# A graph layer and a masked attention layer on one core: block products for the neighbours, one operation for mask and maximum

## The chip, the core and the metric

The kernel runs on one core of a Trainium2 chip. A core has a matrix engine (TensorE, in the profile PE, its weight loads PEld), a vector engine (VectorE, DVE), a scalar engine (ScalarE, ACT), a general engine (GpSimd, POOL) and a queue that issues the transfers (SyncE, SP). Each runs its own instructions in order and waits for the others by semaphores. The metric is the device time of one execution in microseconds.

## The reference, cut to what matters

There are 64 graphs of N = 256 nodes with F = 512 features; all is float32.

```python
# layer 0
deg = jnp.sum(adj, axis=-1, keepdims=True)
agg = jnp.einsum('bij,bjf->bif', adj, x) / jnp.maximum(deg, EPS)
out = relu(jnp.einsum('bnf,of->bno', jnp.concatenate([x, agg], axis=2), W))
x = _layernorm(x + out, axis=-1)
# layer 1, 8 heads of 64, mask = adj + adj
q, k, v = (proj(Wq, bq), proj(Wk, bk), proj(Wv, bv))
scores = jnp.einsum('bhqd,bhkd->bhqk', q, k) * SCALE
attn = jax.nn.softmax(scores * mask, axis=-1)
ctx = jnp.einsum('bhqk,bhkd->bhqd', attn, v)
x = _layernorm(x + jnp.einsum('bse,fe->bsf', ctx, Wo) + bo, axis=-1)
```

The factor 2 of the mask and the scale are folded into the query weights (`QSCALE`), so that the scores are multiplied by `adj` alone.

## The kernel before

A graph's 256 nodes are two tiles of 128 rows (`NT = 2`), its 512 features four chunks. The layer-0 product is turned round: `x W` is computed first, for both halves of W, into the tile `oy` (index 0: the node's own part; index 1: the part `y` that goes to the neighbours), and then `adj y` is divided by the degree and added.

**Products of blocks.** The large products L (`x W`), Q (queries and keys), V (values) and O (output) use a scheme of Winograd's kind: both factors are cut into 2 x 2 blocks, and seven products of blocks take the place of eight. In `winograd`, `product` makes the steps `L1` to `L7` (and so on), which add up in three PSUM banks a, b and c; `kept` makes `Lk5`, `Lk1`, `Lk6`, `Lk4`, which copy a partial sum out of its bank as it stands, and `joined` makes `Lj3`, `Lj2`, `Lj7`, which add one to a part already written. A later product on a bank waits until the partial sum before it has been read. The sums of blocks on the left are made on GpSimd (steps `xS1`-`xS4`, `yS`, `cS`).

**Neighbours.** Step `AY` is the product `adj y`, without that scheme: per tile t two matmuls of 128 x 128 by 128 x 512 into a bank of its own. `AYa` is two VectorE operations: bank times 1/degree plus `oy[:, 0]`, then relu plus x. `AYb`, `AYp`, `AYn` are the layer norm (statistics on VectorE, three small operations on GpSimd, the scaling on ScalarE). `aT` is the transposed `adj`, turned in 32 x 32 blocks on VectorE from the load `Dza`; `xT` comes in the same way from `Dzx`. `Dway`, `Dz1` and `x1T` send the normed x to DRAM, read it back, and turn it for Q and V; `Drest` reads it for the residual, to which `bo` adds the output bias on GpSimd.

**Attention.** The heads go in pairs a, b, c, d. `Sa` is the scores of a pair, into two banks. `ma` multiplies them by `adj`: two VectorE operations of 128 x 512, from PSUM into the tile `sa`. `Ma` is the negated maximum of each row: one VectorE reduction over 128 x 1024. `ea` and `fa` are the exponentials on ScalarE, with the negated maximum as bias and the row sum as a second output; `ra` and `na` divide; `Ta` turns blocks of 32 x 32; `Dwa` and `Dsa` take the weights through DRAM, which completes the transposition; `C0a` (pair a), `C0b` (pair b), `C1a` (pair c), `C1b` (pair d) multiply by v, and `c0`, `c1` copy the context out. `lb`, `lp`, `ln` are the last layer norm and `Dout` the result.

**The order of the work** is written out by hand. `START` lists the steps of the first graphs (name:graph), `PLAN` is one turn of a loop over i = 3 to 59 (name+ahead: the step is made for graph i+ahead), and `END` lists the rest (name:graphs from the end). Every engine gets its instructions in this order. PSUM has eight banks, which all steps take in rotation: a step that takes a new bank waits for the last reader of the bank taken eight before. Most tiles have one buffer only.

Of the kernel before, what the change touches and what calls it, by code (L numbers as in the profile page):

```python
# [35 lines left out]
    AYb1:2 Qk1:1 Q5:1 AYa0:2 nd:0 L5:3 Vj2:1 rc:0 Ta:0 V6:1 nc:0 AYb0:2 Dwa:0 Q6:1 Qj2:1 AYp0:2 Td:0
    Vk6:1 AYp1:2 V5:1 Qk6:1 Tb:0 Dwd:0 L1:3 xS3:3 Vk5:1 yS4:1 Tc:0 Dwb:0 Qk5:1 V7:1 Dwc:0 Q7:1 AYn0:2
    AYn1:2 Q3:1 Qj7:1 Lk1:3 Vj7:1 aT:3 V4:1 deg:3 Dza:4 L6:3 Qj3:1 Dsa:0 Q4:1 Lk6:3 Lk5:3 Dsb:0 Vk4:1
    V3:1 Qk4:1 L7:3 Vj3:1 Drest:0 Dsc:0 Lj7:3 Sa:1 Dsd:0 Sd:1 ma:1 Dway:2 L3:3 Ma:1 md:1 L2:3 ea:1 bo:0
    Lj3:3 fa:1 L4:3 Md:1 Dz1:2 ra:1 Lk4:3 Sb:1 Dadj:4 na:1 Sc:1 mb:1 C0a:0 Lj2:3 fd:1 C1a:0 Mb:1 C1b:0  # L40
    C0b:0 Ta:1 c1:0 eb:1 AY1:3 x1T:2 Dwa:1 Dx:3 c0:0 mc:1 AY0:3 ed:1 yS1:2 Dzx:4 cS3:0 fb:1 O1:0 Wos4:0
    Dadj:5 O2:0 rb:1 yS2:2 aT:4 nb:1 Q1:2 Wos3:0 Mc:1 Q5:2 rd:1 yS4:2 Ok1:0 Qk1:2 AYa1:3 yS3:2 V1:2
    cS1:0 Qk5:2 Tb:1 Q6:2 cS2:0 ec:1 cS4:0 xT1:4 Dwb:1 Q3:2 AYb1:3 Vk1:2 Qk6:2 xT0:4 AYp1:3 O6:0 AYa0:3
    xS1:4 fc:1 V6:2 xS3:4 V5:2 Vk6:2 rc:1 Ok6:0 Q7:2 nc:1 O5:0 Vk5:2 nd:1 Q2:2 Ok5:0 Qj7:2 AYb0:3 O7:0
    Tc:1 AYp0:3 V7:2 xS2:4 O3:0 Oj2:0 Dwc:1 Oj7:0 Q4:2 Vj7:2 Qj3:2 Qj2:2 O4:0 Qk4:2 V3:2 Ok4:0 Oj3:0
    V4:2 AYn0:3 Td:1 Vk4:2 Sa:2 AYn1:3 Vj3:2 Dwd:1 Sc:2 ma:2 Dway:3 Sb:2 Drest:1 Dsc:1 mc:2 Sd:2 L1:4
    Dsb:1 Mc:2 lb0:0 Dsa:1 V2:2 Lk1:4 ec:2 lb1:0 L5:4 lp0:0 Dz1:3 mb:2 lp1:0 fc:2 L6:4 Dsd:1 md:2 xS4:4
# [12 lines left out]
    Sd+0 Dzx+3 Ma+0  # L60
    Sc+0 Dout-2
    C0a-1 mb+0 ea+0
    C1a-1 Dza+2 md+0
    C0b-1 fa+0
    C1b-1 Mb+0 Dz1+1 c1-1
    L5+2 c0-1 mc+0 Dx+2 eb+0 cS3-1
    L1+2 Mc+0 xS2+2 cS1-1 ra+0
    L2+2 Md+0 Lk1+2 xS4+2 Lk5+2 cS2-1 aT+2 fb+0
    L6+2 bo-1
    L3+2 Lk6+2 ec+0  # L70
    O2-1 Lj3+2 na+0
    O1-1
    L7+2 Ok1-1 rb+0 x1T+1 ed+0
    O5-1 Lj7+2 yS1+1 nb+0
    O6-1
    V2+1 Ok6-1 Lj2+2
    L4+2 Ta+0
    V1+1 xT1+3 Lk4+2 Dwa+0 fd+0
    Q1+1 deg+2 xT0+3 fc+0
    O7-1 Tb+0 xS1+3  # L80
    AY0+2 Vk1+1 yS2+1 Oj2-1 Qk1+1 Dwb+0 rc+0 Dsa+0 yS4+1 Ok5-1 Oj7-1
    AY1+2 nc+0 rd+0 cS4-1 xS3+3
    V6+1 AYa1+2 yS3+1 nd+0
    V5+1
    O4-1
    O3-1 Ok4-1 Vk6+1 Tc+0 Vk5+1
    Q6+1 Td+0 Dwc+0
    Q5+1 Qk6+1 Vj2+1 Dwd+0 AYa0+2 Drest+0 Dsb+0
    V3+1 Qk5+1
    V7+1 Vj3+1 Dadj+3 Oj3-1  # L90
    Q7+1 Vj7+1 Dsc+0
    Q3+1 Qj7+1 AYb0+2 Dsd+0
    V4+1 lb0-1 AYp0+2
    Q4+1 lb1-1 Vk4+1 lp0-1 AYn0+2 Qj3+1 lp1-1 AYb1+2
    Q2+1 Qk4+1 AYp1+2 ln1-1 Qj2+1
"""
END = """
    Dza:2 Sb:4 xS2:2 AYn1:3 Sa:4 xS4:2 mb:4 Dway:3 Sc:4 Mb:4 Sd:4 C1a:5 mc:4 fb:4 C0a:5 ma:4 ln0:6 C1b:5
    C0b:5 Dz1:3 md:4 L1:2 Ma:4 Dout:6 L2:2 Lk1:2 Dx:2 eb:4 L5:2 Dzx:1 c0:5 x1T:3 c1:5 L6:2 fa:4 cS1:5
    Mc:4 cS2:5 aT:2 O2:5 Lk6:2 bo:5 fc:4 O5:5 O1:5 Lk5:2 L7:2 ea:4 yS1:3 Ok1:5 yS2:3 L3:2 ec:4 Lj7:2  # L100
    Oj2:5 rc:4 V1:3 Lj2:2 nc:4 Lj3:2 L4:2 rb:4 Ok5:5 Md:4 O6:5 Lk4:2 Vk1:3 Q5:3 Ok6:5 fd:4 Tc:4 V6:3
    ed:4 xT1:1 Dwc:4 AY1:2 ra:4 deg:2 na:4 xT0:1 AY0:2 rd:4 xS3:1 AYa1:2 Qk5:3 yS3:3 Q1:3 cS3:5 AYa0:2
    Vk6:3 yS4:3 V5:3 Qk1:3 xS1:1 O7:5 cS4:5 Vk5:3 V7:3 Oj7:5 nd:4 xS2:1 Ta:4 Q6:3 AYb1:2 Q3:3 Qk6:3
    AYb0:2 AYp1:2 Vj7:3 AYp0:2 Td:4 nb:4 O4:5 Q7:3 Ok4:5 Dwd:4 lb1:5 Dwa:4 AYn1:2 lp1:5 V4:3 Qj7:3 Tb:4
    V3:3 Vk4:3 ln1:5 O3:5 Qj3:3 Dwb:4 AYn0:2 Q4:3 Vj3:3 Dsd:4 Oj3:5 lb0:5 Q2:3 Qk4:3 Dza:1 lp0:5 xS4:1
    ln0:5 Dsc:4 Qj2:3 Sa:3 Sb:3 ma:3 Drest:4 Sd:3 Dsb:4 Ma:3 Sc:3 Dadj:1 L1:1 mc:3 fa:3 Dway:2 Mc:3 L5:1
    Dsa:4 Lk1:1 ea:3 mb:3 Dout:5 L6:1 bo:4 ec:3 aT:1 L2:1 ra:3 Lk6:1 Mb:3 Dx:1 Lk5:1 fc:3 md:3 L7:1
    Dz1:2 na:3 Lj2:1 L3:1 Lj7:1 Md:3 L4:1 Lj3:1 fd:3 rc:3 V2:3 eb:3 Vj2:3 C0a:4 deg:1 Lk4:1 C1a:4 ed:3
    x1T:2 C1b:4 C0b:4 nc:3 yS1:2 AY0:1 yS2:2 c0:4 AY1:1 AYa0:1 c1:4 fb:3 cS3:4 Q1:2 AYa1:1 cS1:4 yS4:2
    Q5:2 yS3:2 Qk1:2 Tc:3 AYb0:1 Q2:2 rb:3 AYp0:1 rd:3 nb:3 O1:4 cS2:4 Qj2:2 O5:4 Ok1:4 Qk5:2 Q6:2 Ok5:4  # L110
    Tb:3 O6:4 Ta:3 Qk6:2 Dwb:3 Q3:2 AYb1:1 Dwa:3 nd:3 Dwc:3 Ok6:4 AYp1:1 Q7:2 Qj3:2 cS4:4 AYn0:1 O7:4
    Qj7:2 AYn1:1 Td:3 Sb:2 Q4:2 mb:2 Dsc:3 Oj7:4 Dwd:3 O3:4 Qk4:2 Mb:2 Dsa:3 O4:4 Oj3:4 eb:2 Dway:1
    Ok4:4 Sa:2 Dsb:3 ma:2 V5:2 fb:2 V1:2 Dsd:3 Ma:2 Vk5:2 V2:2 Vk1:2 lb1:4 fa:2 Sd:2 Drest:3 Dz1:1 md:2
    O2:4 ea:2 V6:2 rb:2 Md:2 Vk6:2 C0a:3 nb:2 Oj2:4 V7:2 lb0:4 V3:2 ra:2 lp0:4 Vj7:2 na:2 Vj2:2 C0b:3
    Tb:2 lp1:4 V4:2 Vj3:2 Vk4:2 x1T:1 C1a:3 fd:2 C1b:3 yS1:1 ln0:4 Sc:2 bo:3 ln1:4 mc:2 Q1:1 c0:3 Dout:4
    c1:3 Mc:2 Q5:1 Qk1:1 yS2:1 Dwb:2 cS1:3 Q6:1 cS2:3 Qk5:1 cS3:3 fc:2 yS4:1 O1:3 cS4:3 Q3:1 Qk6:1 Ok1:3
    Ta:2 yS3:1 ec:2 Q7:1 Qj3:1 Dwa:2 ed:2 rc:2 O6:3 Qj7:1 nc:2 Ok6:3 Sb:1 rd:2 mb:1 O7:3 nd:2 Sa:1 Dsa:2
    Mb:1 O5:3 Tc:2 Q4:1 fb:1 Ok5:3 Dwc:2 Oj7:3 ma:1 Qk4:1 O4:3 Ma:1 eb:1 Q2:1 Td:2 ea:1 O2:3 Ok4:3 Dwd:2
    Qj2:1 fa:1 C0a:2 Drest:2 Dsc:2 rb:1 Sc:1 nb:1 ra:1 Sd:1 Dsb:2 mc:1 O3:3 na:1 lb1:3 Dsd:2 Mc:1 lp1:3
# [11 lines left out]
def kernel(  # L131
# [455 lines left out]
    def score_steps(hp, name):  # L587
# [6 lines left out]
        def of(kind, b):  # L594
            return held[f"{kind}{name}", b]
# [186 lines left out]
```

## Time and profile before

| | |
|---|---|
| three runs | 3089.83, 3091.77, 3093.6 us; median 3091.77 us |
| profiled execution | 3093.68 us, of which the profile's span 3091.9 us |
| mean granted TensorE clock | 0.997 of full speed |
| matmul instructions | 17168, a program matmul on float32 shows as two |
| HBM traffic over the span | 308.55 MB read, 201.33 MB written, 165 GB/s |
| first matmul | 15.86 us after the start, when the first weights have landed |

In what follows, a line such as `L530` is a line of the kernel before. A group line has the operation, output and inputs by the program's names, the count, then busy time in all and the mean of one in ns, then the idle time ahead of it on its engine and what ended it.

### The profile page before, as it was taken

Reading aid. Unit: us, or ns where it says so; the run is one execution under the profiler, and the core shown is the slowest. Engines: PE = TensorE matmul, PEld = TensorE weight load, DVE = VectorE, ACT = ScalarE, POOL = GpSimd, SP = SyncE. Lnnn points to the kernel's source line nnn. Section 1 sums busy time; section 2 is a strip of 40 time slices with the busy share of each in tenths; the row PEclk is TensorE's granted clock in tenths of the full one; section 3 lists DMA queues with packets and bytes.
Section 4 is the critical chain, followed back from the end, with each engine's and each line's share of the span. In section 5 each row is a group of like instructions: output and inputs, shape, how many; then the busy total and the mean of one; then the engine's idle time right before and its main releaser. Section 6 shows DMA issues by size and latency. Waiting matters only on the chain.

```text
span 3091.9 us, 51161 instructions
## 1 busy us (share of the span) xinstructions
PE 3057.1 (99%) x17168; PEld 2262.9 (73%) x17168; DVE 2079.8 (67%) x3594; ACT 1713.5 (55%) x4995; POOL 979.9 (32%) x1677
## 2 busy tenths in 40 slices
PE   7999999999999999999999999999999999999997
PEld 4777777677777776777777777777777777777775
DVE  5666666666666666666666666667666666676674
ACT  2555555555555556555555555555555555555564
POOL 3332333332323333323233333232333333322333
PEclk9999999999999999999999999999999999999998
DMA  8466566565665665756656656557566575565665
GB/s 184 123 181 180 150 175 168 160 182 158 159 183 152 171 171 157 184 156 158 185 154 167 174 154 184 160 155 185 156 163 177 150 184 161 159 183 157 160 167 154
DMA packets 494103, 513.34 MB, mean 166 GB/s; under 512 B 113808, under 2 KB 392336, under 8 KB 493840
## 3 DMA queue, kind: packets, MB, share of 16 engines
q1 hardware_dynamic: 493264, 509.02, 61.6%
q8 instruction: 137, 2.24, 0.3%
q10 hardware_dynamic: 576, 1.05, 0.2%
q14 instruction: 126, 1.03, 0.1%
HBM read 308.55 MB, written 201.33 MB: 165 GB/s over the span
## 4 chain that ended last, share of the span: by engine, by line
PE 97%; DMA 2%; DVE 1%; POOL 0%; SPq 0%; issue 0%; ACT 0%; POOLq 0%; DVEq 0%
PE Qa L462 15%; PE La L435 14%; PE Lc L435 7%; PE pc L688 7%; PE Qc L462 7%; PE Oa L435 7%; PE AY L530 7%; PE Va L435 7%; PE Qb L462 4%; PE Oc L435 4%; PE Vc L435 4%; PE Lb L435 4%; PE sca L605 2%; PE scb L605 2%; PE scc L605 2%; PE Ob L435 2%
## 5 line engine op out<-in xcount | busy, mean ns | idle before, releaser
L478 ACT ACTIVATE qk<-Qa,bqk 128x128 f32<-128x128 f32 x768 | 218.8, 368 | 257.1 <-PE Qa L462 257.0
L451 ACT COPY oy<-La 128x512 f32<-128x512 f32 x192 | 112.3, 585 | 429.6 <-PE La L435 429.6
L516 POOL TENSOR_SCALAR mv<-mv 128x1 f32<-128x1 f32 x256 | 55.8, 218 | 915.1 <-DVE mv L511 884.2
L493 ACT COPY v<-Va 128x256 f32<-128x256 f32 x192 | 70.4, 367 | 340.9 <-PE Va L435 340.9
L376 POOL TENSOR_TENSOR cS<-cT 128x256 f32<-128x256 f32 x128 | 94.1, 735 | 460.4 <-ACT cT L704 460.4
L530 PE MATMUL AY<-oy,aT 128*128 128x512 f32 x512 | 230.8, 593 | 0.0
L503 DVE TENSOR_TENSOR h<-Oa,rest 128x256 f32<-128x256 f32 x192 | 81.4, 424 | 213.8 <-PE Oa L435 209.3
L416 DVE TENSOR_TENSOR oy<-Lc,oy 128x512 f32<-128x512 f32 x64 | 44.2, 691 | 253.8 <-PE Lc L435 248.8
L376 POOL TENSOR_TENSOR yS<-x1T 128x256 f32<-128x256 f32 x128 | 93.7, 732 | 335.0 <-DVE x1T L570 335.0
L376 POOL TENSOR_TENSOR xS<-xT 128x256 f32<-128x256 f32 x128 | 94.5, 739 | 305.3 <-DVE xT L341 273.0
L634 ACT ACTIVATE sa<-sa,nmaxa 128x256 f32<-128x256 f32 x256 | 127.0, 497 | 96.0 <-DVE nmaxa L628 92.4
L542 DVE SCALAR_TENSOR_TENSOR oy<-AY,deg,oy 128x512 f32<-128x512 f32 x128 | 94.8, 741 | 122.0 <-PE AY L530 122.0
L584 POOL TENSOR_TENSOR rest<-rest,bo_sb 128x512 f32<-128x512 f32 x128 | 159.6, 1269 | 29.3 <-DMA rest<-way 29.3
L530 PEld LDWEIGHTS AY<-oy,aT 128*128 128x128 f32 x512 | 96.9, 190 | 96.7 <-issue 91.9
L517 POOL TENSOR_TENSOR mv<-mv,neg_half 128x1 f32<-128x1 f32 x256 | 144.3, 564 | 21.3
L435 PE MATMUL La<-W,xT 128*128 128x512 f32 x256 | 122.6, 602 | 15.9 <-DMA W<-in_w0t_dram 15.9
L634 ACT ACTIVATE sb<-sb,nmaxb 128x256 f32<-128x256 f32 x256 | 128.8, 511 | 3.6 <-DVE nmaxb L628 3.6
L462 PEld LDWEIGHTS Qa<-x1T,Wq 128*128 128x128 f32 x1024 | 124.4, 192 | 6.5 <-DVE x1T L570 1.8
L634 ACT ACTIVATE sd<-sd,nmaxd 128x256 f32<-128x256 f32 x256 | 127.2, 501 | 1.7 <-DVE nmaxd L628 1.7
L634 ACT ACTIVATE sc<-sc,nmaxc 128x256 f32<-128x256 f32 x256 | 127.3, 501 | 1.4 <-DVE nmaxc L628 1.4
L462 PEld LDWEIGHTS Qa<-x1T,Wq_sums 128*128 128x128 f32 x1024 | 124.4, 192 | 3.9 <-issue 0.8
L462 PEld LDWEIGHTS Qa<-yS,Wq 128*128 128x128 f32 x1024 | 124.2, 192 | 3.6 <-issue 0.5
(151 smaller groups left out, 8305.1 us busy)
## 6 DMA issues: line engine op xcount, KB each, us to landing
zx<-in_x_dram SPq DMA_DIRECT2D x256, 128.0 KB, 3.7
x<-in_x_dram SPq DMA_DIRECT2D x256, 128.0 KB, 3.4
way<-x SPq DMA_DIRECT2D x64, 512.0 KB, 3.2
z<-way SPq DMA_DIRECT2D x256, 128.0 KB, 2.9
wsa<-sa SPq DMA_DIRECT2D x64, 512.0 KB, 2.6
wsd<-sd SPq DMA_DIRECT2D x64, 512.0 KB, 3.2
wsb<-sb SPq DMA_DIRECT2D x64, 512.0 KB, 3.0
wsc<-sc SPq DMA_DIRECT2D x64, 512.0 KB, 2.7
```

Of the source, the lines that this page charges most:

```text
L376: nc.gpsimd.tensor_tensor(part_of(s, b, [P, 4, 2, P])[:, k], left(b), right(b), op)
L435: nc.tensor.matmul(ps[:, :width].rearrange("p (m o) -> p m o", o=G), lhsT=left(k, b, c), rhs=w(WEIGHTS[k])[:, :, c], start=first and c == ...
L451: nc.scalar.copy(part_l(b, t, n), ps.rearrange("p (m o) -> p m o", m=2))
L462: nc.tensor.matmul(ps.rearrange("p (m j q) -> p m j q", m=2, j=2)[:, m, j], lhsT=wqk(WEIGHTS[k])[:, m, c, j * P : (j + 1) * P], rhs=left_y ...
L478: nc.scalar.activation(part_q(b, t, n)[:, m, j], ps.rearrange("p (m j q) -> p m j q", m=2, j=2)[:, m, j], AF.Identity, bias=bqk[:, m, c : ...
L517: nc.gpsimd.tensor_tensor(mv[:, 1:2], mv[:, 1:2], neg_half, ALU.pow)
L530: nc.tensor.matmul(ps, lhsT=held["aT", b][:, j, t], rhs=held["oy", b][:, 1, j], start=(j == 0), stop=(j == NT - 1),)
L542: nc.vector.scalar_tensor_tensor(h, held[f"AY{t}", b], rdeg, h, ALU.mult, ALU.add)
L584: nc.gpsimd.tensor_tensor(rest, rest, bo_sb, ALU.add)
L605: nc.tensor.matmul(sc(b, j)[:, t], lhsT=qk[d, 0, hp, t * P : (t + 1) * P], rhs=qk[d, 1, hp].rearrange("d (t b m) -> d b t m", t=NT, m=L), ...
L634: nc.scalar.activation(rows(b)[:, r], rows(b)[:, r], AF.Exp, bias=of("nmax", b)[:, r : r + 1], accum_out=of("total", b)[:, r : r + 1],)
L688: nc.tensor.matmul(ps[j * D : (j + 1) * D, hp % 2], lhsT=held["v", b][:, c, h * D : (h + 1) * D], rhs=held[f"sT{name}", b][:, :, c, j * NT ...
```

## The change

The product `adj y` is cut into blocks as the others are: `adj` into its four 128 x 128 blocks, y into 2 x 2 blocks of 128 x 256. Four sums of blocks of `adj` (`aS1`-`aS4`) and four of y (`bS1`-`bS4`) are made on GpSimd, seven products `Y1` to `Y7` go into two banks (`Ya`, and `Ycb`, whose halves hold the sums c and b), and seven VectorE operations `Yk`/`Yj` scale a partial sum by 1/degree and add it to `oy[:, 0]`. `AYr` keeps the relu and the residual of `AYa`. In the attention, the step m is four operations (one for each row of blocks) that multiply by `adj` and reduce the row to its maximum at once, and M only changes the sign, on GpSimd. The three lists are new.

```diff
+    def adj_block(t, j):
+        return lambda b: held["aT", b][:, j, t]
+    def y_block(j, n):
+        return lambda b: held["oy", b][:, 1, j, n * G : (n + 1) * G]
...
+    def small_sum(name, k, of, left, right, op):
+        steps[f"{name}{k}"] = lambda b: nc.gpsimd.tensor_tensor(of(k)(b), left(b), right(b), op)
+    small_sum("aS", 1, adj_sum, adj_block(1, 0), adj_block(1, 1), ALU.add)
+    small_sum("aS", 2, adj_sum, adj_sum(1), adj_block(0, 0), ALU.subtract)
+    small_sum("aS", 3, adj_sum, adj_block(0, 0), adj_block(1, 0), ALU.subtract)
+    small_sum("aS", 4, adj_sum, adj_block(0, 1), adj_sum(2), ALU.subtract)
+    small_sum("bS", 1, y_sum, y_block(0, 1), y_block(0, 0), ALU.subtract)
+    small_sum("bS", 2, y_sum, y_block(1, 1), y_sum(1), ALU.subtract)
+    small_sum("bS", 3, y_sum, y_block(1, 1), y_block(0, 1), ALU.subtract)
+    small_sum("bS", 4, y_sum, y_block(1, 0), y_sum(2), ALU.subtract)
+    def neighbour_product(k, acc, left, right):
+        @step(f"Y{k}")
+        def _(b):
+            name = "Ya" if acc == "a" else "Ycb"
+            ps = bank(name, b) if k in (5, 1) else held[name, b]
+            nc.tensor.matmul(
+                ps[:, G:] if acc == "b" else ps[:, :G],
+                lhsT=left(b),
+                rhs=right(b),
+                start=k in (5, 1),
+                stop=True,
+                skip_group_check=True,
+            )
+    neighbour_product(5, "c", adj_sum(1), y_sum(1))
+    neighbour_product(1, "a", adj_block(0, 0), y_block(0, 0))
+    neighbour_product(3, "c", adj_sum(4), y_block(1, 1))
+    neighbour_product(6, "a", adj_sum(2), y_sum(2))
+    neighbour_product(2, "b", adj_block(0, 1), y_block(1, 0))
+    neighbour_product(7, "a", adj_sum(3), y_sum(3))
+    neighbour_product(4, "a", adj_block(1, 1), y_sum(4))
+    def neighbour_part(name, acc, t, n):
+        @step(name)
+        def _(b):
+            ps = held["Ya" if acc == "a" else "Ycb", b]
+            h = held["oy", b][:, 0, t, n * G : (n + 1) * G]
+            nc.vector.scalar_tensor_tensor(
+                h, ps[:, G:] if acc == "b" else ps[:, :G], held["deg", b][:, t : t + 1], h, ALU.mult, ALU.add
+            )
...
-        @step(f"AY{t}")
-        def _(b):
-            ps = bank(f"AY{t}", b)
-            for j in range(NT):
-                nc.tensor.matmul(
-                    ps,
-                    lhsT=held["aT", b][:, j, t],
-                    rhs=held["oy", b][:, 1, j],
-                    start=(j == 0),
-                    stop=(j == NT - 1),
-                )
-        @step(f"AYa{t}")
+        @step(f"AYr{t}")
         def _(b):
             h = held["oy", b][:, 0, t]
-            rdeg = held["deg", b][:, t : t + 1]
-            nc.vector.scalar_tensor_tensor(h, held[f"AY{t}", b], rdeg, h, ALU.mult, ALU.add)
             nc.vector.scalar_tensor_tensor(h, h, 0.0, held["x", b][:, t], ALU.max, ALU.add)
...
-            tile_of(f"s{name}", b, [P, A, NT, R, L])
+            s = tile_of(f"s{name}", b, [P, A, NT, R, L])
+            nmax = tile_of(f"nmax{name}", b, [P, R], small, "nmax")
             for j in range(2):
-                nc.vector.tensor_tensor(
-                    rows(b)[:, j * NT : (j + 1) * NT],
-                    sc(b, j).rearrange("p t (k l) -> p t k l", l=L),
-                    held["adj", b].rearrange("p t (k l) -> p t k l", l=L),
-                    ALU.mult,
-                )
+                for t in range(NT):
+                    r = j * NT + t
+                    nc.vector.tensor_tensor_reduce(
+                        out=s[:, :, :, r],
+                        in0=sc(b, j)[:, t].rearrange("p (a c l) -> p a c l", a=A, l=L),
+                        in1=held["adj", b][:, t].rearrange("p (a c l) -> p a c l", a=A, l=L),
+                        scale=1.0,
+                        scalar=-3.4028234663852886e38,
+                        op0=ALU.mult,
+                        op1=ALU.max,
+                        accum_out=nmax[:, r : r + 1],
+                    )
         @step(f"M{name}")
         def _(b):
-            nmax = tile_of(f"nmax{name}", b, [P, R], small, "nmax")
-            nc.vector.tensor_reduce(nmax, rows(b), AX.XY, ALU.max, negate=True)
+            nc.gpsimd.tensor_scalar(of("nmax", b), of("nmax", b), -1.0, None, ALU.mult)
```

The new PLAN whole, the old one cut to its first and last lines; the parts of START and END that the prediction speaks of:

```diff
 PLAN = """
-    Sa+0 AYn1+1
-    Sb+0 ma+0 ln0-2 Dway+1
-    Sd+0 Dzx+3 Ma+0
-    Sc+0 Dout-2
-    C0a-1 mb+0 ea+0
-    C1a-1 Dza+2 md+0
-    C0b-1 fa+0
-    C1b-1 Mb+0 Dz1+1 c1-1
-    L5+2 c0-1 mc+0 Dx+2 eb+0 cS3-1
-    L1+2 Mc+0 xS2+2 cS1-1 ra+0
-    L2+2 Md+0 Lk1+2 xS4+2 Lk5+2 cS2-1 aT+2 fb+0
...
-    Q4+1 lb1-1 Vk4+1 lp0-1 AYn0+2 Qj3+1 lp1-1 AYb1+2
-    Q2+1 Qk4+1 AYp1+2 ln1-1 Qj2+1
+    Sa+0 xS4+2 AYn0+1 Dout-2 Md+0
+    Sb+0 aS1+2
+    C1a-1 Dway+1 mc+0 fd+0
+    C0a-1 ma+0 ed+0
+    C1b-1
+    C0b-1 c1-1 mb+0 c0-1
+    L1+2 cS1-1 rd+0 Dz1+1 Mb+0 cS3-1
+    L5+2 Lk1+2 Ma+0 cS2-1 nd+0 bo-1
+    O2-1
+    L6+2 Lk5+2 Td+0
+    O1-1 Mc+0 cS4-1 Lk6+2 Dwd+0 ea+0
+    L2+2 eb+0
+    L7+2 Lj2+2 deg+2 fc+0
+    L3+2 Dsd+0 Ok1-1 Lj7+2 fa+0 x1T+1
+    O5-1 fb+0
+    O6-1 yS1+1
+    L4+2 Ok6-1 ec+0 Lj3+2 Ok5-1 bS1+2
+    Q1+1 Oj2-1 Lk4+2 ra+0 aS2+2 xT1+3 na+0 bS2+2 xT0+3
+    Y1+2 aS3+2
+    O7-1 Dzx+4 xS3+3
+    O3-1 Oj7-1 bS3+2 Yk1+2 Dx+2
+    Q5+1 rc+0 aS4+2 rb+0 nc+0 Oj3-1 yS3+1 Ta+0 Dza+3 yS2+1
+    V1+1 lb0-1
+    O4-1 Qk1+1 lp0-1
+    Y6+2 Ok4-1
+    Q2+1 Yk6+2 nb+0 yS4+1 Tc+0 bS4+2
+    Y5+2 Dwc+0
+    Q6+1 Yk5+2 Drest+0 Vk1+1 Dwa+0 lb1-1 Tb+0
+    Y2+2 Qk6+1
+    Y7+2
+    Y3+2 Qj2+1 Dwb+0
+    V5+1 Dadj+3 Qk5+1 Yj7+2
+    V6+1 Yj3+2 Yj2+2
+    Q7+1 AYr0+2 Vk6+1 Dsc+0 Vk5+1 Dsa+0
+    Y4+2 Qj7+1
+    V2+1 aT+3
+    V7+1 Dsb+0 Yk4+2
+    Q4+1 AYb0+2 AYr1+2 AYp0+2
+    Q3+1 Vj7+1 Qk4+1 AYb1+2 AYp1+2 ln0-1
+    V3+1 lp1-1
+    V4+1 Vj3+1 Qj3+1 Vk4+1
+    Sd+1 xS1+3 Vj2+1 AYn1+2
+    Sc+1 xS2+3 md+1 ln1-1
...
 START = """
+    bS1:0 Wq:0 Y1:0 aS2:0 Lj7:0 Y5:0 aS4:0 Yk1:0 L4:0 bS2:0 Yk5:0 aS3:0 bS3:0 Y6:0 Lk4:0 xT0:1 Y3:0
+    Yk6:0 Y2:0 bS4:0 xT1:1 Y7:0 Yj7:0 xS1:1 Yj3:0 Y4:0 Yj2:0 xS3:1 L2:1 Yk4:0 AYr0:0 bv2:0 AYb0:0 Dadj:1
...
+    bS2:1 Yk5:1 Wqs1:0 bS3:1 Y6:1 Lk4:1 Yk6:1 Dza:2 bS4:1 x1T:0 Y7:1 Y3:1 Y2:1 Dx:1 Wqs2:0 Q1:0 yS1:0
...
 END = """
+    nc:2 C0b:3 Sb:1 ed:2 mb:1 Q4:1 c0:3 Tc:2 Qk4:1 rd:2 Dwc:2 Mb:1 Dsa:2 nd:2 C1a:3 ma:1 C1b:3 Sc:1 c1:3
+    Ma:1 eb:1 cS1:3 O1:3 Td:2 cS2:3 O5:3 fb:1 cS4:3 Ok1:3 O2:3 Dwd:2 mc:1 Dsc:2 cS3:3 fa:1 Sd:1 Ok5:3
+    Dsb:2 V1:1 Mc:1 ea:1 V2:1 Oj2:3 fc:1 O3:3 ra:1 rb:1 O6:3 md:1 Dsd:2 ec:1 Ok6:3 Oj3:3 O7:3 na:1 lb0:3
+    C0a:2 Oj7:3 lp0:3 Md:1 O4:3 nb:1 Ok4:3 C0b:2 rc:1 Drest:2 lb1:3 V5:1 ed:1 Ta:1 lp1:3 C1a:2 ln0:3
...
```

## The prediction

> **What bounds the kernel.** I read the shares of the engines first, then the chain that ended last, then that chain in order of time inside one turn of the loop, then the groups by shape. Shares, and the chain's shares by engine:
>
> ```profile
> PE 3057.1 (99%) x17168; PEld 2262.9 (73%) x17168; DVE 2079.8 (67%) x3594; ACT 1713.5 (55%) x4995; POOL 979.9 (32%) x1677
> ...
> PE 97%; DMA 2%; DVE 1%; POOL 0%; SPq 0%; issue 0%; ACT 0%; POOLq 0%; DVEq 0%
> ```
>
> TensorE carries 97% of the path, so a change elsewhere counts only if it makes TensorE wait. One turn, from one `sca` to the next (columns: length, busy time of PE, PEld, DVE, ACT, POOL, clock, DMA share, GB/s):
>
> ```profile
> 1536.16:1583.66 47.50, 47.50 (x271) 35.31 (x270) 32.20 (x56) 26.74 (x79) 15.06 (x27) 1.00 0.64 166
> ```
>
> Every `sca` in the loop is 47.50 us behind the last. The chain inside a turn (start, length):
>
> ```profile
> 1515.11 0.86 PE Oa L435 x4
> 1515.97 3.43 PE AY L530 x8
> ...
> 1536.16 1.06 PE sca L605 x8
> 1538.09 0.86 PE scd L605 x8
> 1539.82 3.60 PE pc L688 x32
> 1543.42 1.91 PE Lc L435 x4
> 1545.34 1.72 PE La L435 x4
> ```
>
> Products follow without gaps; only the entries to the scores (1.06 for 0.86), to the context (3.60 for 4 x 0.86) and back to L (1.91 for 1.72) cost more, about 0.55 us a turn together. The new PLAN has the same three entries (Sd Sc Sa Sb over the end of the turn, four C, L1), so that part stays.
>
> **The product, on TensorE.** Removed: AY, eight instructions of 512 columns (512 in the trace for 64 batches), 3.43 us, 0.429 each. Added: seven block products of one matmul. Each program matmul shows as two instructions (4 a batch, 512 in all), so 14 of 128x256. The row for that shape is V or O: 0.862 us for four, 0.2155 each, and 14 x 0.2155 = 3.02. Gain 0.414 us a batch, x64 = **26.5 us**. It is an eighth of 3.43 less 0.01: the shape has no overhead of its own. The weight loads do not come out, because they are shorter than what covers them (190 ns against 215):
>
> ```profile
> L530 PE MATMUL AY<-oy,aT 128*128 128x512 f32 x512 | 230.8, 593 | 0.0
> L416 DVE TENSOR_TENSOR v<-Va,v 128x256 f32<-128x256 f32 x64 | 27.1, 423 | 2.9 <-ACT v L493 0.6 <-PE Va L435 0.2
> L618 DVE TENSOR_TENSOR sa<-sca,adj 128x512 f32<-128x512 f32 x128 | 82.4, 686 | 24.2 <-PE sca L605 24.2
> L628 DVE TENSOR_REDUCE nmaxa<-sa 128x4 f32<-128x1024 f32 x64 | 78.0, 1219 | 2.1
> L542 DVE SCALAR_TENSOR_TENSOR oy<-AY,deg,oy 128x512 f32<-128x512 f32 x128 | 94.8, 741 | 122.0 <-PE AY L530 122.0
> L376 POOL TENSOR_TENSOR yS<-x1T,yS 128x256 f32<-128x256 f32 x64 | 48.0, 749 | 4.5
> L516 POOL TENSOR_SCALAR mv<-mv 128x1 f32<-128x1 f32 x256 | 55.8, 218 | 915.1 <-DVE mv L511 884.2
> L530 PEld LDWEIGHTS AY<-oy,aT 128*128 128x128 f32 x512 | 96.9, 190 | 96.7 <-issue 91.9
> ```
>
> **VectorE.** Removed per batch: the eight mask products (327.7/64 = 5.12 us over the four names), the four reductions (309.5/64 = 4.84), two scaled additions from PSUM (1.48): 11.44. Added: seven scaled additions of 256 columns at 0.741 - 0.267 (slope of 512 to 256 in the rows 686 and 423) = 0.47: 3.3; and 16 fused mask-and-maximum operations of 256 columns, which no row shows. Call one u.
>
> Lower end: two 256-column TENSOR_TENSORs end to end in the tail's timeline start at 3045.39 and 3045.72, so u = 0.33 if the maximum is free. Upper end: 0.42, plus 0.27 for a second pass over 256 columns, plus 0.17 (the smallest VectorE row, a 128x4 RECIPROCAL, 166 ns) to write the maximum out: 0.86. I take 0.52, near the 0.42 row with 0.1 for the write-out. 16 x 0.52 = 8.3, so VectorE goes from 32.2 to 32.4 us a turn (29.4 to 37.8 at the ends) of 47.1, all beside TensorE.
>
> [...]
>
> **Where u would show.** The eight PSUM banks go round in order, so a product waits for the mask that frees its bank. From the start of Sd, TensorE reaches C1a at 3.65 us, L1 at 7.25, L5 at 9.07, O2 at 10.8, O1 at 13.4 and L2 at 14.2 (sums of the pieces above). They need 2, 6, 8, 10, 12 and 14 fused operations done, and VectorE can start at about 1.05 (Sd's end; Vj3, Qj3, Vj2 are through by 0.7). L2 is tightest: (14.2 - 1.05)/14 = 0.94. Up to u = 0.94 nothing waits.
>
> **GpSimd.** Added: four bS (128x256, 0.735), four aS (128x128, about 0.735 less half of the 0.53 from 256 to 512 in the rows 735 and 1269, so 0.47), four negations (0.22): 5.7 us, 15.1 to 20.8 of 47.1. M now waits on POOL for the mask, with cS1 and cS3 ahead of Mb and Ma (0.73 each) and cS, bo and bS queued behind; ScalarE's exponentials wait for M. If all of 1.5 us came late, the weights' transfer would take it: Dsb is issued 12.3 us of TensorE work ahead of C0b and needs some 2.2 to issue and 4.7 to land in the tail's rows. So 5 us are spare; beyond that each us late costs a us per turn.
>
> **Chains and moved steps.** A product waits until the part before it in its bank is drained: Y1 to Y6, Y6 to Y7, Y7 to Y4 have 5.2, 4.4 and 3.9 us of other products between them in PLAN; a drain takes 0.47 plus at most 1.2 of a transpose ahead. SP issues the same transfers. Dza and Dzx move up to a turn ahead (13 us between Dza+3 and aT+3, against 7 before, where it waited 12.6 us in all); Dway, Dz1 and x1T keep 10.3 us from Dz1's issue to x1T's place against 11.9, and z landed in 6.2 us at worst in the tail. Cost nil; if a z transfer took over 10 us, Q1 would wait for it.
>
> **Ends.** In START Y4:0 stands directly behind Y7:0 and Y7:1 behind Y6:1: two stops of about 0.6 (0.47 and the hand-over), +1.2. In END 33 products of 0.86 stand behind the last score Sd:1, where 29 stood: 3.4 us more work under the last head's way to the end (49 us before). But three transfers of four DMAs stand ahead of its last one, and ln0 and ln1 ahead of its exponentials; I take half, -1.5.
>
> Sum: -26.5 + 1.2 - 1.5 = -26.8. The profiled execution took 3093.68 (span 3091.9), so 3066.9; the median of the three runs is 1.9 lower, 3091.77, which gives **3065**.
>
> **Rivals.**
> - Slower: the fused operation holds the banks. [...] It decides from u = 0.97. For it: no row of this operation. Against it: it must be over twice the plain product. 6%.
> - The gain is given back: Y4 or Y7 finds VectorE inside a 1.2 us transpose, or x1T comes late, 0.41 us a turn: 3090, no change. For: VectorE is busy two thirds of the turn, and seven drains of 0.47 replace two. Against: 3.9 us of cover at the least. 4%. A part of it, 0.1 to 0.25 a turn, 3071 to 3080: 10%.
> - More than forecast: the end of before lost 4.4 us to the mask of the last head, and the products after it took 1.9 instead of 0.95 at a lower clock:
>
> ```profile
> 3049.38 1.98 PE L688 MATMUL pc<-sTc,v 128*64 128x256 f32 x8 [4.36 <-DVE sd L618]
> 3051.29 1.97 PE L688 MATMUL pc<-sTb,v 128*64 128x256 f32 x8
> 3053.20 1.95 PE L435 MATMUL Vc<-Wv_sums,yS 128*128 128x256 f32 x4
> ```
>
> In END of after, the bank for C1a:2 waits for Oj3:61, listed 4.3 us of TensorE work ahead, not for a mask. If all 7.3 us go in place of 1.5: 3059. 14%.
>
> The forecast itself has 66%, 3061 to 3071. The range 3057 to 3077 takes in the better end and most of the part given back. Runs differ by 0.1%, so 0.2% (6.2 us) is what can be told from no change: faster 90%, same 4%, slower 6%.
>
> **What would show it.** Right: 47.08 us from score to score in the loop, 896 instructions for the new product at 0.2155, no wait of PE for VectorE in mid-run, DVE busy 1900 to 2400 us, POOL near 1340. Wrong: a wait at L2, O2 or L5 ended by the fused mask, Y products longer than 0.43, or a loop at 47.08 with ends that differ by more than 5 us.

## The result, and the profile after

| | before | after |
|---|---|---|
| three runs, median | 3091.77 us | 3069.96 us (3067.2 to 3070.47) |
| profiled execution, of it the span | 3093.68, 3091.9 us | 3069.96, 3068.2 us |
| mean granted TensorE clock | 0.997 | 0.998 |

The ratio is 0.9928, with a 95% interval of 0.9909 to 0.9948: 21.8 us less by the medians, 23.7 by the profiled executions. The forecast was 3065, in a range of 3057 to 3077.

First the page of after: the shares of the engines, and the chain's shares.

```profile
PE 3031.2 (99%) x17552; PEld 2324.1 (76%) x17552; DVE 1897.9 (62%) x5194; ACT 1689.5 (55%) x4995; POOL 1341.2 (44%) x2445
...
PE 98%; DMA 1%; DVE 0%; ACT 0%; SPq 0%; issue 0%; POOL 0%; POOLq 0%; DVEq 0%; ACTq 0%
```

TensorE carries the path as before, with 384 instructions more (896 of the new product for 512 of the old). VectorE lost 182 us of busy time and GpSimd gained 361; neither is on the chain. One turn of the loop, from one `scd` to the next (the columns as in the prediction):

```profile
1528.14:1575.23 47.09, 47.09 (x276) 36.27 (x275) 29.40 (x82) 26.32 (x78) 20.74 (x39) 1.00 0.62 168
```

47.09 us where 47.50 stood, TensorE busy through all of it, VectorE at 29.4 and GpSimd at 20.7. The groups by shape show the new operations one by one:

```profile
L553 POOL TENSOR_TENSOR yB<-oy 128x256 f32<-128x256 f32 x128 | 94.3, 736 | 111.1 <-DVE oy L429 105.5 <-DVE totalb L721 5.3 <-DVE totalc L721 0.2
L593 DVE SCALAR_TENSOR_TENSOR oy<-Ya,deg,oy 128x256 f32<-128x256 f32 x256 | 119.6, 467 | 9.8 <-PE Ya L571 9.1
L690 DVE CUSTOM_DVE_ANT_0 sa<-sca,adj 128x256 f32<-128x256 f32 x256 | 93.0, 420 | 3.1 <-PE sca L674 3.1
L690 DVE DVE_READ_ACCUMULATOR2_ANT nmaxa<- 128x1 f32 x256 | 21.3, 83 | 0.0
L703 POOL TENSOR_SCALAR nmaxd<-nmaxd 128x4 f32<-128x4 f32 x64 | 14.9, 232 | 49.0 <-DVE nmaxd L690 49.0
```

The fused mask and maximum is a `CUSTOM_DVE_ANT_0` of 0.42 us and a read-out of the maximum of 0.08. What counts in a row of sixteen is how they follow each other, and that is in the timeline of VectorE (start, length):

```profile
1529.65 0.42 DVE L690 CUSTOM_DVE_ANT_0 sd<-scd,adj 128x256 f32<-128x256 f32 x1
1530.00 0.09 DVE L690 DVE_READ_ACCUMULATOR2_ANT nmaxd<- 128x1 f32 x1
1530.00 0.42 DVE L690 CUSTOM_DVE_ANT_0 sd<-scd,adj 128x256 f32<-128x256 f32 x1
```

The next operation starts together with the read-out of the one before, 0.345 us after that one's start on the mean of the sixteen (1529.30 to 1534.82).

The loop is as forecast; what is missing lies at its edge. The timeline of TensorE in the first turn (graph 2's context, just behind START):

```profile
211.63 1.08 PE L763 MATMUL pc<-sTd,v 128*64 128x256 f32 x8 [0.43 <-DMA sTd<-wsd]
214.38 1.98 PE L763 MATMUL pc<-sTb,v 128*64 128x256 f32 x8 [1.67 <-DMA sTb<-wsb]
216.28 2.65 PE L448 MATMUL La<-W,xT 128*128 128x512 f32 x4
```

Two waits for the attention weights, 2.1 us, and then products that are too long: 2.65 for an L that takes 1.98 at this place of later turns. That turn lasts 51.19 us (205.59 to 256.78), 4.1 more than the rest; before has no wait there, and its first turn takes 47.50. The chain of waits in order of time says what stood ahead:

```profile
203.19 6.14 DMA rest<-way
209.33 0.02 issue
209.35 4.89 DMA sTb<-wsb
```

`rest` is the residual of the same graph, 512 KB that GpSimd takes up only at 219.49, when it adds the bias. It is issued at 203.19, ahead of the reads of pairs d (203.67) and b (205.91).

The tail has the same pattern, in the timeline of TensorE:

```profile
3045.17 1.08 PE L763 MATMUL pc<-sTc,v 128*64 128x256 f32 x8 [1.46 <-DMA sTc<-wsc]
3049.37 1.97 PE L763 MATMUL pc<-sTd,v 128*64 128x256 f32 x8 [3.12 <-DMA sTd<-wsd]
```

The 4.36 us for the last mask that before shows are gone. In their place stand these two waits for transfers, 0.93 us for a copy of v and 1.43 for a copy of the context.

### The profile page after: what moved, and what is told of

The parts are those of the page before. It is cut to its first block, busy times and chain, and to the rows that moved or that the text cites. A ratio compares the mean times of both kernels' runs of the same rounds, so it can differ in the third digit from the quotient of the medians.

```text
span 3068.2 us, 54922 instructions
## 1 busy us (share of the span) xinstructions
PE 3031.2 (99%) x17552; PEld 2324.1 (76%) x17552; DVE 1897.9 (62%) x5194; ACT 1689.5 (55%) x4995; POOL 1341.2 (44%) x2445
## 3 DMA queue, kind: packets, MB, share of 16 engines
q10 hardware_dynamic: 576, 1.05, 0.2%
## 4 chain that ended last, share of the span: by engine, by line
PE 98%; DMA 1%; DVE 0%; ACT 0%; SPq 0%; issue 0%; POOL 0%; POOLq 0%; DVEq 0%; ACTq 0%
PE La L448 15%; PE Qa L475 15%; PE Qc L475 7%; PE pc L763 7%; PE Oa L448 7%; PE Lc L448 7%; PE Va L448 7%; PE Qb L475 4%; PE Lb L448 4%; PE Ya L571 4%; PE Oc L448 4%; PE Vc L448 4%; PE Ycb L571 3%; PE scd L674 2%; PE Ob L448 2%; PE Vb L448 2%
## 5 line engine op out<-in xcount | busy, mean ns | idle before, releaser
L529 POOL TENSOR_SCALAR mv<-mv 128x1 f32<-128x1 f32 x256 | 77.6, 303 | 769.3 <-DVE mv L524 756.8
L733 DVE STREAM_TRANSPOSE sd<-sd 128x1024 f32<-128x1024 f32 x64 | 79.6, 1244 | 273.4 <-ACT sd L726 273.4
L429 DVE TENSOR_TENSOR oy<-Lb,oy 128x512 f32<-128x512 f32 x64 | 44.2, 691 | 209.3 <-PE Lb L448 202.4
L726 ACT ACTIVATE sc<-sc,totalc 128x256 f32<-128x256 f32 x256 | 109.3, 497 | 106.7 <-DVE totalc L721 106.7
L553 POOL TENSOR_TENSOR yB<-oy 128x256 f32<-128x256 f32 x128 | 94.3, 736 | 111.1 <-DVE oy L429 105.5
L709 ACT ACTIVATE sd<-sd,nmaxd 128x256 f32<-128x256 f32 x256 | 127.0, 497 | 24.5 <-POOL nmaxd L703 24.4
L779 ACT COPY cT<-pc 128x512 f32<-128x512 f32 x128 | 74.9, 586 | 116.3 <-PE pc L763 116.3
L448 PE MATMUL Lb<-W,xT 128*128 128x512 f32 x256 | 122.2, 600 | 15.6 <-DMA W<-in_w0t_dram 15.6
```

Of the source, the lines that this page charges most:

```text
L448: nc.tensor.matmul(ps[:, :width].rearrange("p (m o) -> p m o", o=G), lhsT=left(k, b, c), rhs=w(WEIGHTS[k])[:, :, c], start=first and c == ...
L553: steps[f"{name}{k}"] = lambda b: nc.gpsimd.tensor_tensor(of(k)(b), left(b), right(b), op)
L709: nc.scalar.activation(rows(b)[:, r], rows(b)[:, r], AF.Exp, bias=of("nmax", b)[:, r : r + 1], accum_out=of("total", b)[:, r : r + 1],)
L726: nc.scalar.activation(rows(b)[:, r], rows(b)[:, r], AF.Identity, scale=of("total", b)[:, r : r + 1])
```

## The experiments

Times are set against the kernel before on the same chip: 3092.2 us (31 runs) for e1, e2, e3 and e6, 3090.74 (9 runs) for e4, e5 and e8, 3091.55 (9 runs) for e9, e10 and e11. e4, e5 and e9 are one execution each.

### Is it the product or the mask?

Three kernels take the two halves apart. **e1_old_mask** is after with the mask and the maximum of before:

```diff
-                    nc.vector.tensor_tensor_reduce(out=s[:, :, :, r], ..., op1=ALU.max, accum_out=nmax[:, r : r + 1])
+                nc.vector.tensor_tensor(rows(b)[:, j * NT : (j + 1) * NT], ..., ALU.mult)
...
-            nc.gpsimd.tensor_scalar(of("nmax", b), of("nmax", b), -1.0, None, ALU.mult)
+            nc.vector.tensor_reduce(nmax, rows(b), AX.XY, ALU.max, negate=True)
```

> The changed kernel with the mask and the maximum of before (eight mask products and four reductions a batch on VectorE), product by blocks and lists as changed. Theory (TensorE bounds every turn, the mask part is hidden): 47.09 us from score to score in the loop as in the changed kernel, VectorE busy about 2.6 us a turn more, time within 3 us of the changed kernel's 3070. Rival (relief of VectorE is worth something): the turn goes back toward 47.2 to 47.5 and waits of TensorE for VectorE show at L2 or O2.

3069.18 us (ratio 0.9925, 0.991 to 0.9939), level with after. One turn, in the columns used above:

```profile
1528.14:1575.23 47.09, 47.09 (x278) 36.27 (x276) 33.29 (x61) 26.30 (x79) 19.86 (x35) 1.00 0.63 168
```

VectorE works 3.9 us more in a turn and TensorE doesn't notice. **e2_old_product** is after with AY at the place of Y4, no sums of blocks, and the lists otherwise those of after:

```diff
-    Q5+1 rc+0 aS4+2 rb+0 nc+0 Oj3-1 yS3+1 Ta+0 Dza+3 yS2+1
+    Q5+1 rc+0 rb+0 nc+0 Oj3-1 yS3+1 Ta+0 Dza+3 yS2+1
...
-    Y4+2 Qj7+1
+    AY0+2 AY1+2 Qj7+1
...
-    Q4+1 AYb0+2 AYr1+2 AYp0+2
+    Q4+1 AYa0+2 AYr0+2 AYb0+2 AYp0+2
```

> The changed kernel with the neighbours' product of before (two products of 512 columns a batch, both at the place of Y4, no sums of blocks), mask and lists otherwise as changed. Theory: 47.50 us a turn, 26.5 us more than the changed kernel, 3096 give or take 5. Rival (the new order of steps carries part of the gain): under 3085 and a turn under 47.4.

3097.13 us (ratio 1.0017, 1.0011 to 1.0024):

```profile
1446.94:1494.44 47.50, 47.50 (x270) 35.13 (x269) 28.26 (x77) 26.30 (x78) 16.38 (x31) 1.00 0.62 168
```

The turn is back at 47.50: the seven products are the whole gain of the loop. The run is also 4.9 us slower than before with the same work on TensorE; its first scores of the loop start at 211.67 us, where before has 206.19 and after 205.59. START in the new order thus costs the old product 5.5 us. **e3_mask_alone** is before, lists included, with the fused operation and the sign on GpSimd:

> The kernel before with only the fused mask and maximum and the sign on GpSimd, lists of before. Theory: 47.50 us a turn, 3092 give or take 3, although VectorE is busy some 2.6 us a turn less. Rival (VectorE's relief counts): 47.4 or less a turn, 3085 or less. Other rival (the sign on GpSimd comes late): above 47.6 a turn, with C waiting for sT.

3091.17 us (ratio 0.9995, 0.9986 to 1.0003), the turn still 47.50 (`sca` at 1441.43 and 1488.93). Taken alone, without the product, the mask part changes nothing either.

### How long may the fused operation be?

The prediction said that nothing waits until it takes 0.94 us. **e4_mask_twice** and **e5_mask_thrice** issue each of them two and three times:

```diff
-                    nc.vector.tensor_tensor_reduce(
+                    for _ in range(2):
+                        nc.vector.tensor_tensor_reduce(
```

> The kernel after with each fused mask-and-maximum operation issued twice in a row; the second computes the same again, so nothing else changes. In the trace of after these operations follow each other at 0.345 us, so the pair takes u = 0.69 for each row of blocks, and VectorE rises from 29.4 to about 34.9 us a turn. My theory (PSUM banks bind only from u = 0.94): L2 needs 1.05 + 14 x 0.69 = 10.7 us and comes at 14.2, so nothing waits; turn 47.09, time within 6 us of after's 3070. Rival (a full VectorE delays the chain from the scores to the weights and the scaled additions long before any bank is late): the turn rises by 0.2 us or more, 3082 or above, and TensorE waits for transfers sT or for parts of Y.

> The kernel after with each fused mask-and-maximum operation issued three times in a row, the same result each time; nothing else changes. u = 3 x 0.345 = 1.035, above the 0.94 from which the prediction said that banks bind. My theory: L2 then waits 1.05 + 14 x 1.035 - 14.2 = 1.3 us a turn, ended by the mask, and VectorE is at about 40.5 us a turn; with 57 turns 3070 + 75 to 90 = 3145 to 3160, with the waits of TensorE at L2, O2 or L5 put down to the mask. Rival (the banks have more room than the sum says, since VectorE begins earlier or the pairs' second halves come free sooner): turn 47.1 to 47.3, under 3085. Second rival (the weights' chain is late first): waits at C0 and C1 for the transfers sT, not at L2.

3146.85 us for two and 3696.7 for three. My theory fell twice: two should have cost nothing and took 1.2 us a turn (48.32), and three took 10.4 us in some two turns of three (57.48) and 8.7 in the others (55.79), where some 1.3 to 1.6 was expected. The 1.7 us between the two kinds of turn are a lower clock (0.97 on the mean of the turn for 1.00), shown in the last section. The rival for two had the size and not the place: TensorE waits neither for the transfers nor for parts of Y.

One error was the length. In the timeline of VectorE the operations of e4 start at 1565.44, 1565.91, 1566.26 and 1566.72: one that repeats the one before it starts 0.465 us after it, not 0.345. So u was 0.81 in e4 and 1.28 in e5 (sixteen rows from 1547.56 to 1568.04). That alone doesn't explain e4, for L2 then needs 1.05 + 14 x 0.81 = 12.4 us and comes at 14.3. The waits of TensorE in e4 name another place (us in all, times, longest):

```profile
PE La L448 <- ACT oy L464: 49.8, 57, 1.0
```

Not a bank that the mask holds, but a copy by ScalarE of a part of L. The timeline of ScalarE in e4:

```profile
1578.65 1.70 ACT L728 ACTIVATE sd<-sd,totald 128x256 f32<-128x256 f32 x4 [4.37 <-DVE totald L723]
1580.26 0.56 ACT L464 COPY oy<-Lc 128x512 f32<-128x512 f32 x1
1580.73 0.58 ACT L464 COPY oy<-La 128x512 f32<-128x512 f32 x1
```

ScalarE stood still for 4.37 us in front of the division of pair d (`nd`), which waits for the reciprocal `rd`. On VectorE `rd` is listed behind the four masks. Behind `nd` stand the copies Lk5 and Lk6, whose sources had long been ready and without which the bank can't take its next product. In after `nd` starts 9.8 us behind Sd (1537.95), and in e4 14.4. The waits of TensorE in e5 show both mechanisms:

```profile
PE La L448 <- ACT oy L464: 191.6, 58, 5.0
PE pc L765 <- issue: 84.0, 57, 1.5
PE Lb L448 <- DVE nmaxb L691: 80.4, 56, 1.4
PE Ob L448 <- DVE nmaxa L691: 34.7, 57, 0.7
PE Lc L448 <- DVE nmaxc L691: 26.5, 58, 1.5
```

The banks bind at L5 (`Lc`), O2 (`Ob`) and L2 (`Lb`), the places that the prediction named. The wait of `pc` that has no releaser is a fourth, C0a, which the prediction left out: it takes the second bank of pair d and so needs four operations done. The timelines of VectorE and of TensorE, with the last operation on pair d and C0a:

```profile
356.94 0.42 DVE L691 CUSTOM_DVE_ANT_0 sd<-scd,adj 128x256 f32<-128x256 f32 x1
```

```profile
357.47 1.08 PE L765 MATMUL pc<-sTa,v 128*64 128x256 f32 x8 [1.47 <-issue]
```

C0a starts 0.11 us after the operation's end. The copy behind `nd` costs more than any one bank, 3.3 us a turn; these four banks together cost 3.9. **e9_twice_div_late** puts the new theory to the test:

```diff
-    L5+2 Lk1+2 Ma+0 cS2-1 nd+0 bo-1
+    L5+2 Lk1+2 Ma+0 cS2-1 bo-1
     O2-1
-    L6+2 Lk5+2 Td+0
-    O1-1 Mc+0 cS4-1 Lk6+2 Dwd+0 ea+0
+    L6+2 Lk5+2
+    O1-1 Mc+0 cS4-1 Lk6+2 nd+0 Td+0 Dwd+0 ea+0
```

> The kernel of the run with each fused operation issued twice, with one thing moved in PLAN: the division and the block transposition of pair d (nd and Td) stand behind the copy Lk6 instead of ahead of Lk5. In the run without the move a turn took 48.32 us, and TensorE waited 0.88 us in each for the copy of a part of L. My new theory: the sixteen fused operations last 13.0 us there (0.81 for a pair, not 0.69); the reciprocal rd stands behind them on VectorE, nd on ScalarE waits for rd, and the copies Lk5 and Lk6, which free the bank for the next L, are queued behind nd. With nd moved they no longer wait, no bank is late (L2 needs 1.05 + 14 x 0.81 = 12.4 us and comes at 14.3), and the turn is 47.1 to 47.2 again: 3074 to 3085 in all, since START and END keep their order. Rival (VectorE's 13 us block is late for other work too, the rows' sums on GpSimd or the parts of L that it adds): the wait only goes to another place and the turn stays at 48 us or more, 3130 to 3150.

3082.25 us, 65 less than e4 with the same instructions. It is 12 over after, of which 57 turns make 5; the rest lies in START and END, which keep the order of e4. Its ScalarE timeline and its turn:

```profile
1542.17 0.59 ACT L464 COPY oy<-Lc 128x512 f32<-128x512 f32 x1 [1.08 <-PE Lc L448]
1544.75 0.59 ACT L464 COPY oy<-La 128x512 f32<-128x512 f32 x1 [1.99 <-PE La L448]
1545.46 1.71 ACT L728 ACTIVATE sd<-sd,totald 128x256 f32<-128x256 f32 x4
```

```profile
1531.08:1578.26 47.18, 47.18 (x276) 36.50 (x275) 36.21 (x114) 26.52 (x78) 20.76 (x39) 1.00 0.63 167
```

The copies now wait for TensorE and no longer TensorE for them. With VectorE at 36.2 us a turn and u = 0.81, the turn is back to within 0.09 us, so the order of ScalarE's queue was the cause in e4. The 0.09 us arise ahead of L1, which comes 7.35 us behind Sd where after has 7.26: C0a comes at 4.61 for 4.57, 0.12 us after the fourth operation on pair d has ended, so its bank begins to bind at this u.

### The residual ahead of the weights

**e6_rest_late** moves one transfer of after, behind the pair that it delayed:

```diff
-    lb0:1 Dsc:2 AYr1:4 lp0:1 Dsa:2 V7:3 Qj7:3 V3:3 AYr0:4 Drest:2 Q4:3 Vj7:3 Dsd:2 Qj2:3 AYb1:4 V4:3
-    Qk4:3 Dsb:2 lb1:1 ...
+    lb0:1 Dsc:2 AYr1:4 lp0:1 Dsa:2 V7:3 Qj7:3 V3:3 AYr0:4 Q4:3 Vj7:3 Dsd:2 Qj2:3 AYb1:4 V4:3
+    Qk4:3 Dsb:2 Drest:2 lb1:1 ...
```

> The changed kernel with one step moved in START: the reload of the residual of graph 2 (Drest:2) stands behind Dsb:2 instead of ahead of Dsd:2. Theory (the first turn of the loop lost 4.1 us because the 512 KB reload went ahead of the weights that C1b and C0b wait for): the first turn falls from 51.2 to 47.1 to 48 us, no wait for sTd or sTb there, 3 to 4 us off the whole, about 3066. Rival (that stretch is bound by the traffic of all transfers, whatever their order): the first turn stays at 50 or more, no change in time.

3066.72 us (ratio 0.9915, 0.99 to 0.993). The first turn takes 47.96 us for 51.19, and one of its waits is left, in the timeline of TensorE:

```profile
213.56 1.08 PE L763 MATMUL pc<-sTb,v 128*64 128x256 f32 x8 [0.64 <-DMA sTb<-wsb]
214.58 1.98 PE L448 MATMUL La<-W,xT 128*128 128x512 f32 x4
```

The L behind it has its usual 1.98 us. START came to its end at 206.45, 0.9 us later than in after, but that is within what one kernel shows: e10 below is after unchanged and has 207.06. The other traces agree on the order of the two transfers: with `Drest` ahead the first turn takes 50.30 us in e1 and 49.22 in e10, with it behind 47.08 in e8 and 47.69 in e11. **e8_rest_late_twice** makes the same move in the tail as well:

```diff
-    Ok6:2 Oj2:2 ... Ok4:2 lb0:2 Drest:1 Dsd:1 lb1:2 lp0:2
+    Ok6:2 Oj2:2 ... Ok4:2 lb0:2 Dsd:1 Drest:1 lb1:2 lp0:2
```

> The kernel after with the two residual reads moved in SP's order: the one of graph 2 in START stands behind the transfers of pair b (as in the run with that move alone, 3066.7 us), and the one of the last graph in END stands behind the transfers of the last pair d. In the run with the first move alone, SP issued the last residual read at 3039.09 when VectorE's first layer-norm step let its buffer go, and the four reads of pair d only from 3039.57 to 3041.4, although SP was free at 3038.19; they landed 5.2 us after the last issue and TensorE waited 2.55 us. My theory: the four reads go out 1.4 us earlier and share the engines with no 512 KB read, so that wait falls to about 0.5 to 1.1 us and the run to about 3064.5 to 3065.5, ahead of both kernels. Rival: the residual is then late for the last output sum, or the products after it simply start earlier and wait at the layer norm of graph 2 instead: no change against 3066.7.

3063.49 us (ratio 0.9915, 0.9901 to 0.9929). In the tail, by the timeline of TensorE:

```profile
3041.45 1.08 PE L763 MATMUL pc<-sTc,v 128*64 128x256 f32 x8 [1.19 <-DMA sTc<-wsc]
3043.91 1.65 PE L763 MATMUL pc<-sTd,v 128*64 128x256 f32 x8 [1.38 <-DMA sTd<-wsd]
```

The wait for pair d fell from 2.55 to 1.38 us, not as far as expected. From the start of the last graph's first C to the end it is 23.4 us, where e6 has 26.0. By the ratios e6 and e8 can't be told apart, so the second move alone is shown by the traces only; after and e8 were put on one chip, **e10_after_again** and **e11_late_twice_again**, unchanged:

> The kernel after, unchanged, for a comparison on one chip with the next run. Expected 3068 to 3072 us and a ratio of 0.992 to 0.994 to before.

> The kernel with both residual reads moved behind the transfers that TensorE waits for, on the same chip as the kernel after. By the traces the two moves bring 3.2 us at the seam of START and loop, less 0.9 us of later START, and 2.6 us in the tail, so it should be 4.5 to 6.5 us under the kernel after. Rival (chips and single executions differ by as much): the two are within 2 us of each other.

3068.05 us (3066.78 to 3068.89) and 3064.15 (3063.7 to 3065.66); the ratios to before are 0.9924 (0.9911 to 0.9936) and 0.9913 (0.99 to 0.9927). The version with both moves is 3.9 us faster than after, with no overlap of the five runs each; 4.5 to 6.5 was expected. The two profiled executions differ by 4.7: the first turn by 1.5 (49.22 and 47.69), the tail from the last graph's first C by 2.6 (24.4 and 21.8), the end of START by 0.8. So the tail gave what the traces had promised, and the first turn gave less than the 3.2 us between after and e6. Two waits are left in the tail of e11, in the timeline of TensorE:

```profile
3044.67 1.08 PE L763 MATMUL pc<-sTd,v 128*64 128x256 f32 x8 [1.26 <-DMA sTd<-wsd]
...
3048.94 1.13 PE L448 MATMUL Oc<-Wo_sums,cS 128*128 128x256 f32 x4 [1.26 <-POOL cS L389]
```

The second is for the block sums cS, which are queued behind the bias of the residual on GpSimd (from 3045.71). In e8 it is absent: there the three products ahead took 1.65, 2.07 and 1.21 us for 1.08, 1.13 and 1.03 here, and cS was ready in time. To list the bias behind cS in the tail would be the next step; it wasn't tried.

## Why the prediction was right, and where it was off

The forecast was 26.8 us from the profiled execution, of which 23.7 came. Term by term, from the two traces: a turn is 47.497 us in before and 47.087 in after, on the mean of 56 turns, and of the 64 products five fall into START and two into END.

| term | forecast | measured |
|---|---|---|
| seven products for eight, 64 batches | -26.5 | -26.2 |
| START, two stops | +1.2 | +1.4 |
| first turn of the loop | not in the sum | +4.1 |
| END | -1.5 | -3.0 |
| sum | -26.8 | -23.7 |

- **The product.** Right to 0.01 us a turn: 47.08 forecast, 47.09 measured, and e2 gives 47.50 back. The three entries to scores, context and L stayed in the turn as said, and none of the seven drains is waited for in the loop.
- **START.** The stops came at Y4:0 and Y7:1 as predicted, 0.67 us each. The profile puts the first down to a sum on GpSimd, but VectorE's drain ended 0.15 us before the product began, as at the second.
- **The seam of START and loop** is the term that failed. The prediction worked out that Dsb has 5 us to spare, but from PLAN, where it is issued 12.3 us of TensorE work ahead of C0b. For graph 2 that step stands in START's last lines, with about 8 us of work ahead and `Drest:2` in the queue. Of the 4.1 us, 2.1 are the waits and 1.6 a lower clock behind them (0.63 of full speed for 4.4 us). That `Drest` is the cause is shown by e6, where that one transfer is moved and 3.2 us are gone; how much it costs differs, since e10, the same kernel as after, lost 2.1 us there and not 4.1.
- **END** gained twice what was taken. The mask's wait went, as the better-ends rival said, but two waits for transfers, of pairs c and d, take 4.6 us where before has 2.3, and the prediction had them only as "three transfers stand ahead of its last one". e8 and e11 show part of that to be the place of `Drest:1`. The half that the prediction took was a guess, and it is luck that its error of 1.5 us made up for part of the seam's.
- **The fused operation** was taken at u = 0.52 and measured 0.345, near the lower end of 0.33. The maximum costs almost nothing. VectorE as a whole has 29.4 us to do in a turn where before has 32.2, and e1 and e3 show that this moves no time (47.09 us a turn with the new product and 47.50 with the old, under either mask). The upper end, 0.86, was an estimate from rows of before, with 0.27 for a second pass and 0.17 for the write-out; in the run neither holds up the next operation. Where the sources lie made little difference in before, in operations without the second output: 716 ns with both float32 sources in SBUF, where the mask's product of 512 columns with one source in PSUM took 680 to 686:

```profile
L543 DVE SCALAR_TENSOR_TENSOR oy<-oy,x 128x512 f32<-128x512 f32 x128 | 91.7, 716 | 4.4
```

- **"Up to u = 0.94 nothing waits"** was wrong, and harmless only because u was small. The sum of the banks left out C0a, which by the prediction's own pieces comes at about 4.55 and needs four operations: 0.88, tighter than L2. Measured, C0a comes at 4.57 and the operations start at 1.16; with the 0.07 us by which the fourth outlasts its step and the 0.12 to C0a's start, that bank binds from about 0.80, an estimate. And the banks were not the first limit: `nd` and with it Lk5 and Lk6 wait for the end of the sixteen operations. From e4 (0.88 us late at u = 0.81) that limit is near 0.81 - 0.88/16 = 0.76, an estimate too. At the prediction's own upper end of 0.86 the change would have been slower than before, since e4 at 0.81 already is; the rival for that side had the right sign, but in e4 the wait is for the copy and not, as it said, for a bank that the mask holds; in e5 the banks add theirs. The list of what is queued behind the mask named M on GpSimd and the exponentials, and left out the reciprocal and the division.
- **The last 1.9 us** of the difference is no mechanism. The forecast was brought down from the profiled execution of before to its median; after's profiled execution lies at its own median.

## What to carry to other kernels

When a longer operation is said to be hidden, follow every in-order queue behind it to the next thing that TensorE needs, not only the buffers that it holds: here the limit was a copy of an unrelated product, two queues on. Where steps are software-pipelined, work out the spare time of a transfer once for the loop and again for the first and last turn, where a hand-made list places it otherwise. A large transfer that nothing needs soon belongs behind the small ones that TensorE waits for, and what is queued behind its consumer must be looked at too.

## What the runs showed of the hardware

- The maximum that is fused into the mask's product is nearly free in a row of such operations on VectorE: 0.345 us from start to start with the maximum, against 0.33 for a plain sum of 256 columns (3045.39 and 3045.72 in before), since the 84 ns of read-out lie under the next operation. The same operation repeated on the same outputs follows only after 0.465 us; what holds it, the runs don't show.
- A short wait of TensorE was followed by a loss of nearly its own length in after (2.1 us of waits, 1.6 of a lower clock), and not in e10. Windows over the products behind the seam's waits, for after and then for e10 (the last columns are clock, DMA share, GB/s):

```profile
214.40:218.80 4.40, 4.40 (x13) 2.05 (x14) 0.00 (x0) 0.59 (x1) 1.75 (x4) 0.63 0.89 273
```

```profile
213.00:221.00 8.00, 6.64 (x29) 3.67 (x30) 2.21 (x14) 4.42 (x12) 3.78 (x7) 1.00 0.84 209
```

After waited 2.1 us there and e10 1.7. After was granted 0.63 of the clock for 4.4 us, which is 1.6 us more; e10 kept the full clock, and its first turn took 49.22 us where after's took 51.19. The same kernel thus differs by 2 us at this place from one execution to the next. The length of the wait doesn't decide it: e1 waited 2.8 us there, and the L behind the waits took its usual 1.98 us (first turn 50.30). In the tail the clock was 0.52 in before for the 5.77 us behind the wait of 4.36, and 0.58 in after for the 5.63 us behind the wait of 3.12. In e5 two turns that follow each other have the same waits to 0.01 us, the longest of them 3.29 us; behind it the clock fell in the first of the two and not in the second:

```profile
1546.40:1603.88 57.48, 50.05 (x275) 36.76 (x275) 43.24 (x146) 26.20 (x78) 20.76 (x39) 0.97 0.56 142
1603.88:1659.67 55.79, 48.36 (x276) 36.19 (x275) 43.13 (x146) 26.20 (x78) 20.75 (x39) 1.00 0.52 143
```

What sets it off can't be told from these traces.
